# Two graph layers on one core: when the next batch of x is loaded, and into which buffer

## The chip, the cores and the metric

The kernel runs on one core of a Trainium2 chip. The metric is the device time in microseconds of that core, the median of three runs. A profiled execution was taken beside them; all stage times below are from it, and it was itself longer than the timed runs (1170.05 us against 1118.38 us).

## The reference

The input x is 32 batches of 512 nodes by 512 features, in float32. Two residual layers run one after the other, each with a layer norm and a ReLU in front.

```python
# --- layer 0 ---
h = jnp.maximum(_layernorm(x, axis=-1), 0.0)
y = jnp.einsum('nm,bmd->bnd', adj, h)
x = x + jnp.einsum('bnd,do->bno', y, weight) + bias
# --- layer 1 ---
h = jnp.maximum(_layernorm(x, axis=-1), 0.0)
q, k, v = h @ Wq + bq, h @ Wk + bk, h @ Wv + bv          # 8 heads of 64
scores = einsum('bqhd,bkhd->bhqk', q, k) / sqrt(64) + (1.0 - adj) * -1e9
out = einsum('bhqk,bkhd->bqhd', softmax(scores), v)
x = x + out.reshape(b, n, d) @ Wo + bo
```

The mask term is so large that, where each row of adj has a single largest entry, the softmax picks exactly one key for each query. Then layer 1 comes down to: take row idx(n) of h, multiply by Wv Wo, and add it to row n of x.

## The kernel before

The kernel first looks at adj and the weights on the chip and takes `single_path` if the softmax is sure to pick one key per row; with these inputs it does, and the other path plays no part in the time.

Work goes batch by batch, in a loop over b from 0 to B. Each turn of the loop runs three stages one after the other on TensorE. Each is one product of two 512 x 512 matrices by a scheme with seven products of half-sized blocks instead of eight (`product`, pieces p1, p5, u2, c11, c22, c12, c21):

- layer 0 of batch b (`layer0`, steps 0 to 6): y times w0, added onto x by VectorE (`take_onto`, L344),
- aggregation for batch b + 1 (`aggregate`, steps 7 to 13): adj times h, moved to yT by ScalarE and VectorE (L326, L324),
- layer 1 of batch b - 1 (`layer1`, steps 14 to 20): Wv Wo times the distinct rows that any query picked (352 columns), moved to zs (L337, L334).

Pieces of one product share accumulators. u2 and then c22 are added into the bank of p1, so the matmuls of c22 may start only when VectorE has taken u2 out of the bank (L344). That wait is the one named `PE mm L287 <- DVE x L344` below.

All other work hangs on these 21 steps by hand. `put(batch, step, f)` appends f to a step of this turn, and every engine runs its own instructions strictly in that order. Around the change:

- The results of layer 1 go back through memory. `put_z` (L545, L549) transposes zs and writes 11 groups of 32 rows to a buffer z in memory, in eight DMAs, at step 20 of one turn and step 0 of the next. `finish` (L553, step 1) adds the rows onto x with four indirect DMAs issued by GpSimd. `store` (L559, step 12) writes x to the output.
- The way out to layer 1 goes through memory too: `put_h` (L488, steps 9 and 11) writes h, `get_h` (L494, steps 12 and 15) gathers the picked rows with 11 indirect DMAs issued by GpSimd, and the next turn transposes them (`transpose_h`, L529, steps 5 to 8).
- GpSimd also computes the reciprocal square roots of the norms (`power`, L201), in the same queue as its DMAs.
- x lives in five buffers, batch b in `xs[b % 5]`. `load_x` (L253) issues four DMAs of 256 KB on the SyncE queue. The norm of batch b + 2 (`stats`, L194) reads the loaded x from step 9 on.

SyncE's queue carries, in one turn and in this order: the second half of z (step 0), the load of x, the two writes of h, the four stores, the first half of the next z (step 20). A DMA that must wait for another holds up all that stand behind it in the queue.

Of the kernel before, what the change touches and what calls it, by code (L numbers as in the profile page):

```python
# [26 lines left out]
def gnn_two_layers(ctx: ExitStack, tc: tile.TileContext, x, adj, w0, b0, wq, bq, wk, bk, wv, bv, wo, bo, out):  # L27
# [149 lines left out]
    with tc.If(single > P - 1) as cmp:  # L177
        single_path(tc, x, wv, bv, wo, bo, out, kept)
# [38 lines left out]
def single_path(ctx: ExitStack, tc: tile.TileContext, x, wv, bv, wo, bo, out, kept):  # L217
# [361 lines left out]
    with tc.manual_schedule():  # L579
# [6 lines left out]
        for b in range(B + 1):  # L586
            todo = [[] for _ in range(21)]

            def put(batch, step, f, *args):
                if 0 <= batch < B:  # L590
                    todo[step].append(lambda: f(batch, *args))

            put(b - 2, 15 if b == B - 1 else 1, finish)
            put(b + 2, 2, load_x)
            for step, i in ((0, 0), (1, 1), (2, 2), (3, 3)) if b > 0 else ((1, 0), (2, 1), (2, 2), (3, 3)):
                put(b + 1, step, h0_sum, i)
            put(b - 2, 14 if b == B - 1 else 0, put_z, 0, 6)
# [347 lines left out]
```

## Time and profile before

| What | Value |
|---|---|
| Timed runs | 1115.33, 1118.38, 1119.31 us; median 1118.38 us |
| Profiled execution | 1170.05 us, of which the trace spans 1168.3 us |
| TensorE (PE) busy | 1100.6 us, 94% of the span |
| VectorE (DVE) busy | 905.7 us, 78% |
| GpSimd (POOL) busy | 653.9 us, 56% |
| ScalarE (ACT) busy | 359.4 us, 31% |
| Granted TensorE clock, mean | 0.984 |
| DMA moved | 186.90 MB, mean 160 GB/s |

"Busy" is the time in which an engine has an instruction under way. A wait is written as who waited, an arrow, and what came last before it went on; "SPq" is the queue of SyncE, which only issues DMAs. In the tables by stretch, each engine's busy time and its number of instructions are followed by the granted clock, the busy share of the 16 DMA engines, and the rate that they moved.

### The profile page before, as it was taken

How to read it: one execution, taken by the hardware profiler on the slowest of the kernel's cores; microseconds unless marked ns; L12 is line 12 of the kernel's file. 1: busy time of each engine (PE TensorE's matmuls, PEld its weight loads, DVE VectorE, ACT ScalarE, POOL GpSimd, SP SyncE). 2: the span in 40 equal slices, each digit the busy share in tenths (PEclk: the TensorE clock that was granted, in tenths of full speed). 3: DMA queues.
4: the chain of work that ended last, by engine and by line, in shares of the span. 5: the costliest groups of instructions: out<-in, count | busy, mean ns of one | idle time of the engine just before them, and what ended most of it. 6: DMA issues, size and time to landing. Idle time of an engine off the chain costs nothing.

```text
span 1168.3 us, 15855 instructions
## 1 busy us (share of the span) xinstructions
PE 1100.6 (94%) x5408; PEld 957.8 (82%) x5408; DVE 905.7 (78%) x1859; ACT 359.4 (31%) x655; POOL 653.9 (56%) x584
## 2 busy tenths in 40 slices
PE   7999989999989999999999999899999999999885
PEld 3658878989978989888989888798998889998782
DVE  6879868878867878787888888687887878887760
ACT  4223313233313233323323332223333232233120
POOL 2146536655646765565765555566565656666443
PEclk9999989999989999999999999999999999999998
DMA  6414665655666665576665657566566756666438
GB/s 225 153 19 129 165 173 140 171 170 149 168 173 139 165 180 147 153 191 167 150 177 171 159 155 187 133 170 178 155 165 172 190 140 167 180 176 156 120 118 203
DMA packets 135146, 186.90 MB, mean 160 GB/s; under 512 B 17472, under 2 KB 61120, under 8 KB 135056
## 3 DMA queue, kind: packets, MB, share of 16 engines
q1 hardware_dynamic: 102320, 123.05, 31.0%
q0 software_dynamic: 29472, 56.47, 27.4%
q10 hardware_dynamic: 3264, 6.29, 1.5%
q8 instruction: 44, 0.72, 0.2%
q14 instruction: 46, 0.38, 0.1%
HBM read 96.28 MB, written 89.46 MB: 159 GB/s over the span
## 4 chain that ended last, share of the span: by engine, by line
PE 83%; DVE 6%; issue 3%; POOL 3%; ACT 1%; DMA 1%; another core or an unknown queue 1%; SPq 0%; POOLq 0%; ACTq 0%; DVEq 0%
PE mm L287 78%; DVE x L344 2%; POOL x L553 1%; PE mm L139 1%; PE mm L480 1%; PE mm L371 1%; DVE st L194 1%; DMA x<-in_x_dram 1%; PE mm L520 1%; ACT h L212 1%; POOL rstd L201 1%; POOL hc L494 1%; DVE h0s L266 1%; DVE yT L324 0%
## 5 line engine op out<-in xcount | busy, mean ns | idle before, releaser
L494 POOL DMA_INDIRECT hc<-hs,listed x341 | 356.2, 1045 | 261.9 <-DMA hs<-h 157.2
L344 DVE TENSOR_TENSOR x<-mm,x 128x512 f32<-128x512 f32 x217 | 149.6, 690 | 146.6 <-PE mm L287 107.7
L326 ACT COPY yT<-mm 128x512 f32<-128x512 f32 x124 | 71.8, 579 | 614.3 <-PE mm L287 478.3
L553 POOL DMA_INDIRECT x<-z,place x124 | 196.0, 1581 | 70.2 <-issue 47.9
L287 PE MATMUL mm<-w_t,sel 128*128 128x256 f32 x744 | 182.2, 396 | 37.9 <-DVE x L344 31.6
L212 ACT ACTIVATE h<-x,off,rstd 128x512 f32<-128x512 f32 x256 | 194.7, 807 | 48.2 <-DVE off L204 46.3
L287 PEld LDWEIGHTS mm<-w_t,sel 128*128 128x128 f32 x744 | 143.9, 196 | 67.5 <-DVE x L344 39.4
L201 POOL TENSOR_TENSOR rstd<-ve,mhalf 128x2 f32<-128x2 f32 (+1 forms) x97 | 97.2, 1002 | 156.9 <-DVE ve L200 151.8
L194 DVE BATCH_NORM_STATS2 st<-x 128x6 f32<-128x512 f32 x256 | 171.6, 670 | 8.4 <-DMA x<-in_x_dram 7.3
L287 PE MATMUL mm<-adjT_s,h0s 128*128 128x256 f32 x744 | 170.9, 379 | 0.4 <-ACT yT L326 0.2
L287 PEld LDWEIGHTS mm<-adjT_s,h0s 128*128 128x128 f32 x744 | 141.2, 190 | 20.3 <-ACT yT L326 1.2
L287 PE MATMUL mm<-hTs,wvo_t 128*128 128x176 f32 x720 | 117.8, 313 | 1.7 <-ACT zs L337 1.7
L287 PE MATMUL mm<-w_s,yT 128*128 128x256 f32 x496 | 117.2, 379 | 0.0
L287 PE MATMUL mm<-adjT,h 128*128 128x256 f32 x496 | 117.2, 379 | 0.0
L337 ACT ACTIVATE zs<-mm,cvo_c 128x176 f32<-128x176 f32 x248 | 87.4, 404 | 94.7 <-PE mm L287 60.4
L287 PEld LDWEIGHTS mm<-hTs,wvo_t 128*128 128x128 f32 x720 | 109.7, 190 | 2.8 <-ACT zs L337 2.8
L287 PEld LDWEIGHTS mm<-adjT,h 128*128 128x128 f32 x496 | 94.2, 190 | 13.2 <-issue 0.5
L287 PEld LDWEIGHTS mm<-w_s,yT 128*128 128x128 f32 x496 | 93.1, 190 | 11.7 <-issue 0.5
L458 DVE TENSOR_TENSOR x<-x,b_r 128x512 f32<-128x512 f32 x128 | 86.5, 677 | 0.0
L287 PE MATMUL mm<-hT,wvo 128*128 128x176 f32 x480 | 81.4, 313 | 0.0
L287 PEld LDWEIGHTS mm<-hT,wvo 128*128 128x128 f32 x480 | 75.3, 190 | 1.5
L324 DVE TENSOR_TENSOR yT<-mm,yT 128x512 f32<-128x512 f32 x93 | 63.5, 682 | 4.1 <-PE mm L287 2.7
(152 smaller groups left out, 1262.9 us busy)
## 6 DMA issues: line engine op xcount, KB each, us to landing
hs<-h SPq DMA_DIRECT2D x64, 512.0 KB
out_dram<-x SPq DMA_DIRECT2D x124, 256.0 KB
x<-in_x_dram SPq DMA_DIRECT2D x120, 256.0 KB
z<-zr SPq DMA_DIRECT2D x124, 96.0 KB
z<-zr SPq DMA_DIRECT2D x124, 80.0 KB
hc<-hs,listed POOLq DMA_INDIRECT x341
x<-z,place POOLq DMA_INDIRECT x124
x<-in_x_dram ACTq DMA_DIRECT2D x4, 256.0 KB
```

The source lines that it names most:

```text
L139: nc.tensor.matmul(ps, hs[0][:, m, d * P:(d + 1) * P], adjT[:, m, :], start=(m == 0), stop=(m == C - 1))
L194: self.nc.vector.bn_stats(st, self.src[:, self.chunks[i], :])
L201: self.nc.gpsimd.tensor_tensor(self.rstd, ve, self.mhalf[:, 0:n], ALU.pow)
L212: self.nc.scalar.activation(dst, src, AF.Relu, bias=self.off[:, i:i + 1], scale=self.rstd[:, i:i + 1])
L287: nc.tensor.matmul(bank[:, m, 0:half], lhs[:, k, m * P:(m + 1) * P], rhs[:, k, :], start=(first and m == 0 and k == 0), stop=(k == 1), ski ...
L324: nc.vector.tensor_add(dst, bank, dst)
L326: nc.scalar.copy(dst, bank)
L337: nc.scalar.activation(dst[:, m, :], bank[:, m, :], AF.Identity, bias=cvo_c[:, 2 * i + m:2 * i + m + 1])
L344: nc.vector.tensor_add(dst, bank, dst)
L458: nc.vector.tensor_add(X[b][:, c, :], X[b][:, c, :], b0_r)
L494: nc.gpsimd.indirect_dma_start(out=HC[b][:, s, :], out_offset=None, in_=HS[b].rearrange("n (q d) -> (n q) d", q=4), in_offset=bass.Indirec ...
L553: nc.gpsimd.indirect_dma_start(out=X[b][:, c, :], out_offset=None, in_=Z[b], in_offset=bass.IndirectOffsetOnAxis(ap=place[:, c:c + 1], axi ...
```

## The change

The load moves from step 2 to step 15 of the loop's turn, and fetches batch b + 3 instead of b + 2. Batch b + 3 goes into `xs[(b + 3) % 5]`, the buffer that batch b - 2 has just left at step 12, so each DMA of the load now follows the store of the same buffer by three steps; before, eleven steps lay between the two (the store at step 12, the load into that buffer at step 2 of the following turn). It is meant to take the load out of the stretch in which z is written and added onto x, and to put it where the DMA engines have less to do. The first two turns still load at step 2 as well, since nothing has been stored by then.

```diff
             put(b - 2, 15 if b == B - 1 else 1, finish)
-            put(b + 2, 2, load_x)
+            if b < 2:
+                put(b + 2, 2, load_x)
+            if b > 0:
+                put(b + 3, 15, load_x)
```

What is loaded, where it is kept, and all other work stay as they are. In the instruction order of the engines, only SyncE's differs: the four loads stand after the four stores instead of after z. VectorE keeps its order; its transpose before z (L545, the first half) waits for eight DMA semaphores in place of four.

## The prediction

> **What bounds the kernel now.** I read the clock view first (mean 0.984, so the clock is nearly full), then the engines' shares (TensorE 94%), then the table by stretch with one turn of the loop per row, because a mean over the span hides whether TensorE lacks work in every turn or in some.
>
> ```profile
> core 0: us, PE busy (x) PEld busy (x) DVE busy (x) ACT busy (x) POOL busy (x), PEclk, DMA share, GB/s
> 216.60:249.10 32.50, 32.50 (x170) 29.60 (x169) 27.27 (x57) 10.80 (x20) 20.11 (x18) 1.00 0.66 172
> 249.10:286.00 36.90, 34.53 (x171) 30.78 (x170) 27.58 (x57) 11.10 (x21) 21.18 (x19) 0.95 0.60 156
> 286.00:318.50 32.50, 32.50 (x170) 29.53 (x169) 27.59 (x57) 10.91 (x20) 21.11 (x18) 1.00 0.68 174
> 318.50:357.50 39.00, 35.92 (x171) 31.63 (x170) 27.76 (x57) 10.93 (x20) 20.09 (x18) 0.91 0.57 145
> 143.30:1073.90 930.60, 896.55 (x4538) 805.17 (x4537) 744.85 (x1513) 295.06 (x540) 556.44 (x486) 0.99 0.63 164
> ```
>
> The reader is to see two kinds of turn. In the good ones TensorE is busy for all of the 32.5 us: the turn is TensorE's own work and nothing else. The bad ones last 37 to 39 us with the same instructions. The last row holds 27 turns (4538 matmul records at 168 a turn): 930.6 / 27 = 34.47 us each, so 27 x (34.47 - 32.5) = 53 us of the profiled span are lost in bad turns.
>
> Next, where a bad turn loses it. The waits of TensorE between 143.3 and 1073.9 us, and the timeline of the bad turn that starts at 249.1:
>
> ```profile
> PE mm L287 <- DVE x L344: 27.4, 12, 3.2
> PE mm L287 <- issue: 6.2, 3, 3.8
> ```
>
> ```profile
> 250.86 3.62 PE L287 MATMUL mm<-w_t,sel 128*128 128x256 f32 x16
> ...
> 253.56 1.91 SPq L253 DMA_DIRECT2D x<-in_x_dram  x4
> ...
> 254.94 0.69 DVE L344 TENSOR_TENSOR x<-mm,x 128x512 f32<-128x512 f32 x1 [2.59 <-PE mm L287]
> ...
> 257.83 0.69 DVE L344 TENSOR_TENSOR x<-mm,x 128x512 f32<-128x512 f32 x1 [1.60 <-remote]
> ...
> 258.58 3.00 PE L287 MATMUL mm<-w_t,sel 128*128 128x256 f32 x8 [2.37 <-DVE x L344]
> ```
>
> TensorE waits for VectorE, yet VectorE is itself idle: it waits 2.59 us for TensorE. The 16 matmuls from 250.86 on are p5 (eight) and u2 (eight); at 0.216 us from start to start, p5's last one ends near 250.86 + 8 x 0.216 + 0.16 = 252.75. VectorE gets the word at 254.94, over 2 us later, and the one of u2 at 257.83 although u2 was over near 254.5. "remote" is what the view writes when no instruction ended shortly before. So the word of the matmuls' end comes late; no engine is short of time. The half-clock stretches follow such waits (0.95 and 0.91 in the two bad rows) and make up the rest of the 53 us.
>
> **Is this in the timed runs?** The profiled execution took 1170.05 us, the timed median is 1118.38: 51.7 us less. The bad turns account for 53 us. Taking them out of the profiled time gives 1170.05 - 53 = 1117, within 1.4 us of the timed median. I therefore hold that the timed runs have almost none of these late words, and that they spend their 27 middle turns at TensorE's 32.5 us.
>
> Last, where the load stands among the transfers of a good turn's worth of time:
>
> ```profile
> 515.57 2.43 SPq L488 DMA_DIRECT2D hs<-h  x2
> 518.10 2.67 SPq L559 DMA_DIRECT2D out_dram<-x  x4
> 530.83 3.77 SPq L549 DMA_DIRECT2D z<-zr  x8
> 534.64 1.90 SPq L253 DMA_DIRECT2D x<-in_x_dram  x4
> ```
>
> ```profile
> 519.00:523.00 4.00, 4.00 (x22) 3.64 (x21) 3.93 (x10) 0.59 (x1) 1.45 (x2) 1.00 0.93 349
> 523.00:531.00 8.00, 8.00 (x55) 7.92 (x54) 7.48 (x15) 5.53 (x12) 6.56 (x7) 1.00 0.17 46
> 531.00:537.00 6.00, 6.00 (x29) 5.29 (x28) 2.89 (x5) 0.23 (x1) 4.66 (x5) 1.00 0.74 196
> 537.00:541.00 4.00, 2.51 (x12) 1.89 (x11) 2.93 (x6) 0.00 (x0) 1.72 (x1) 1.00 0.72 242
> 541.00:549.00 8.00, 8.00 (x39) 7.04 (x38) 7.25 (x17) 2.12 (x4) 5.40 (x4) 1.00 0.85 124
> ```
>
> The load now follows z and falls between 535 and 541, just ahead of the four accumulating DMAs of `finish` (541 to 549, 0.85 busy). From 523 to 531, in layer 1, the DMA engines are 0.17 busy. The change moves 1 MB from the crowded stretch into that hole.
>
> **What the Trainium skill says.** "DMA: Bandwidth & Descriptors", section "Issuing engines are not separate DMA queues": transfers from SyncE and GpSimd run on the same 16 DMA engines and interleave. The trace agrees: one busy share covers z, x and the gathers, and GpSimd's indirect DMA takes 1.42 us beside the load at 290.35 where it takes 0.95 us without. The same page, section "Two DMAs through the same engine are not ordered": a DMA that depends on an earlier one has to wait, on the issuing engine, for that one's semaphore, so queue order alone isn't enough. This is the wait that the load will have on the store; the trace of before can't show it, since no load there waits so. "TensorE: Matmul & The Clock Gate", section "Part 1: The HAM clock gate": the clock goes to half after a window of about 3.4 us in which TensorE was idle. The trace shows half clock right after TensorE's waits of 2 to 3 us, so it agrees roughly: waits somewhat shorter than the page's window were enough.
>
> **The change, part by part.**
>
> Removed at step 2: four DMA issues, 1.90 us of SyncE's queue, which is idle from 536.5 to 549.5 anyway. The 1 MB leaves the DMA engines before `finish`. GpSimd waits 2.27 us ahead of the first DMA of `finish` (539.15 against the last gather's end at 536.9). With z's last DMA issued at 534.16 and nothing behind it, z should land up to 2 us sooner, so `finish` may start near 537 and end near 545 instead of 546.5. Who gains: the reciprocal roots (L201) behind it in GpSimd's queue, and VectorE, which waits for them 33.6 us in 42 waits in the middle turns. But TensorE waited only 2.0 us in all for the VectorE work behind that (L324). Worth to the end: 0 to 2 us.
>
> Added at step 15: the load waits in SyncE's queue for each store to land. The stores are issued from 518.1 to 520.8 and the fast traffic ends near 523; the Trainium skill's DMA page ("Anatomy of one DMA") puts about 2 us of fixed cost on a transfer, so as an estimate the first lands at 521 to 522 and the last at 523 to 525. Issues then run to about 525 or 526 and, at the 349 GB/s of the row above, 1 MB takes 3 us: landed by 530. Behind the load in the queue stands only the first half of z, ready at 530.8. It is not held up: 5 us of room. If the stores took twice as long, still 2.
>
> Moved into the hole: the 11 gathers run from 521.2 to 536.9 beside it. At 1.42 - 0.95 = 0.47 us more for the six issued in those 8 us, that is up to 2.8 us later on GpSimd; those issued beside the load at step 2 today get it back (three in the turn at 286). Net 0 to 1.5 us, against the 2.27 us that GpSimd idles before `finish`: hidden. The last gather is needed by the third transpose at 513.4 in the turn before, 547 in this one, some 9 us after its issue: hidden.
>
> The data: read from step 9 of the next turn on instead of seven steps after its issue. VectorE doesn't wait for x in the middle turns today, so the longer lead is worth nothing. The four more semaphores on L545 cost VectorE an instruction or two of 0.05 us (the length of the ones that it has now), before p1 is taken; u2 can start only after that, with about 0.8 us to spare in the good turn (p1 taken by 288.61, u2's first matmul at 287.72 + 8 x 0.216 = 289.45). Hidden.
>
> Sum on the path of the timed run: minus 0 to 2 us, plus 0. I take 1.9 us, most of the upper end, since some late words may be left in the timed runs as well.
>
> **The rivals.**
>
> Faster by over 0.5%: the late words are caused by the crowd of z, gathers and x, and the timed runs still have some. For it: they come in layer 0's first pieces, just where z is written, turn after turn. Against it: in the turn shown, the word of p5 was late before the first load was issued (253.56), so z and not x would be the cause, and z stays; and the room is small. 1170.05 - 53 leaves 1.4 us; if the profiled head and tail hold losses too (the last 94 us have a mean clock of 0.92, some 7 us), the room is 1.4 + 7 = 8 us. All of it: 1118.4 - 8 = 1110 us.
>
> Slower by over 0.5%: the gathers and the load disturb each other more than 0.47 us a DMA, `finish` starts later, the roots behind it come late, VectorE stops in front of them with layer 0's pieces and aggregation's behind, and TensorE follows. For it: VectorE is over 0.9 busy in layer 1 and has little room to catch up. Against: 2.27 us of slack at `finish`. If 0.3 us a turn got through: 28 x 0.3 = 8 us, 1127 us; at 1 us a turn, 1146 us.
>
> Slower by SyncE: the load's wait for the store holds z. That needs 5 us more than estimated; each further us would then come onto z and `finish`. For 1 us a turn again 1146 us; I give it little.
>
> **How the numbers follow.** No measurable change 0.56: the prediction, 1118.4 - 1.9 = 1116.5 us. Faster by over 0.5% (below 1112.8) 0.31, centred on 1110. Slower by over 0.5% (above 1124) 0.13, both slower rivals together. The range from 1106 to 1124 leaves out half of the extreme end of the faster case and nearly all of the slower ones, about 2 in 10.
>
> **What would show it.** Right: the load issued between 521 and 526 on the same scale (some 6 us after the stores begin), the DMA share of the hole near 0.5, `finish` starting up to 2 us sooner after z, no wait of VectorE for x, and good turns still at 32.5 us. Bad turns may become fewer in the profiled run without the timed ones following. Wrong: good turns of other than 32.5 us; a timed gain beyond 8 us, which would mean that the late words are in the timed runs too; or z issued late behind the load, or GpSimd's roots late behind gathers that take over 1.4 us.

## The result, and the profile after

The changed kernel takes 1112.97 us (median; 1112.71 to 1113.45), the kernel before beside it 1118.65 us (1115.33 to 1119.31). The ratio is 0.9956 with a 95% interval from 0.9936 to 0.9976: a gain of 0.44%, clear of noise, and just inside the half per cent that was called no measurable change (the interval reaches to both sides of it). 1116.5 us was predicted. In this text, medians are of all runs and ratios of the fast ones alone (at most 1.5% above the fastest of their kernel); for chip D below, where most runs are slower than that, the median of the fast ones is given.

The profiled execution of the changed kernel took 1112.71 us, 57 us less than that of the kernel before (1170.05 us). That is not the effect of the change. The experiments below show that one and the same kernel differs by this much from one group of runs to another, each group on its own chip. So the two profiles can be compared in the order and the places of their transfers, but not in their length, nor in how often TensorE waits.

By stretch (length, busy time and count of each engine, clock, DMA share, rate), a turn of the loop and the 27 middle turns of the changed kernel:

```profile
699.30:731.90 32.60, 32.60 (x171) 29.67 (x170) 27.69 (x57) 10.92 (x20) 21.06 (x18) 1.00 0.66 174
142.00:1024.60 882.60, 881.27 (x4537) 798.12 (x4537) 744.28 (x1513) 294.81 (x540) 565.19 (x487) 1.00 0.66 172
```

882.6 / 27 = 32.69 us a turn, so what the middle turns lose against 32.5 us is 5 us in all. The waits of TensorE in the middle turns say the same; of the 27.4 us for L344 nothing is left:

```profile
PE mm L287 <- ACT yT L326: 0.3, 1, 0.3
```

This is not the work of the change: on another chip the changed kernel still waits 25.4 us for L344 (below).

SyncE's queue over one turn (start, length, what):

```profile
488.56 2.44 SPq L488 DMA_DIRECT2D hs<-h  x2
491.09 2.67 SPq L559 DMA_DIRECT2D out_dram<-x  x4
494.15 2.67 SPq L253 DMA_DIRECT2D x<-in_x_dram  x4
503.80 3.79 SPq L549 DMA_DIRECT2D z<-zr  x8
```

The load starts 3.1 us after the stores do, and z follows 7 us after the load's last issue. The queue's own waits show what the new dependence costs it:

```profile
SPq L253 <- DMA out_dram<-x: 46.8, 104, 2.0
```

That is 46.8 / 104 = 0.45 us for each of the load's DMAs that waited, at most 2.0, in a stretch where nothing else stands in the queue. And the DMA engines by stretch, to be set beside the stretches of before in the prediction:

```profile
494.00:499.00 5.00, 5.00 (x34) 4.90 (x33) 4.93 (x12) 2.50 (x7) 4.14 (x4) 1.00 1.00 349
499.00:503.50 4.50, 4.50 (x31) 4.45 (x30) 4.00 (x8) 3.36 (x6) 3.39 (x5) 1.00 0.20 61
503.50:510.00 6.50, 6.50 (x32) 5.72 (x31) 5.48 (x9) 0.48 (x2) 5.28 (x5) 1.00 0.61 161
```

The hole behind the stores is filled (share 1.00 from 494 to 499), the stretch of z has dropped from 0.74 to 0.61. In layer 0 the words of the matmuls' end come on time in this profile:

```profile
505.16 0.65 DVE L344 TENSOR_TENSOR x<-mm,x 128x512 f32<-128x512 f32 x1
...
506.72 0.69 DVE L344 TENSOR_TENSOR x<-mm,x 128x512 f32<-128x512 f32 x1 [0.32 <-PE mm L287]
...
508.45 0.69 DVE L344 TENSOR_TENSOR x<-mm,x 128x512 f32<-128x512 f32 x1 [0.44 <-PE mm L287]
```

p1, p5 and u2 are taken 1.6 to 1.7 us apart, the pace of eight matmuls (8 x 0.216). In the bad turn of before it was 3.9 and 2.9 us; there p1 was taken at 251.08, and p5 and u2 at 254.94 and 257.83, as the prediction shows:

```profile
251.08 0.67 DVE L344 TENSOR_TENSOR x<-mm,x 128x512 f32<-128x512 f32 x1
```

### The profile page after: what moved, and what is told of

Same layout as the page of the kernel before. It is cut to its first block, busy times and chain, and to the rows that moved or that the text cites. A ratio compares the mean times of both kernels' runs of the same rounds, so it can differ in the third digit from the quotient of the medians.

```text
span 1110.9 us, 15992 instructions
## 1 busy us (share of the span) xinstructions
PE 1083.0 (97%) x5408; PEld 950.4 (86%) x5408; DVE 905.1 (81%) x1859; ACT 359.2 (32%) x655; POOL 662.4 (60%) x584
## 4 chain that ended last, share of the span: by engine, by line
PE 87%; DVE 5%; POOL 2%; issue 2%; DMA 1%; ACT 1%; SPq 0%; POOLq 0%; ACTq 0%; DVEq 0%
PE mm L287 83%; PE mm L139 1%; POOL x L553 1%; PE mm L480 1%; DVE st L194 1%; PE mm L371 1%; POOL rstd L201 1%; DVE x L344 1%; DMA x<-in_x_dram 1%; DVE yT L324 1%; DVE zs L334 0%; SPq L549 0%; DMA z<-zr 0%; ACT zs L337 0%; DVE mv L195 0%
## 5 line engine op out<-in xcount | busy, mean ns | idle before, releaser
L494 POOL DMA_INDIRECT hc<-hs,listed x341 | 367.7, 1078 | 261.1 <-DMA hs<-h 156.2
L326 ACT COPY yT<-mm 128x512 f32<-128x512 f32 x124 | 71.5, 577 | 546.0 <-PE mm L287 489.7
L553 POOL DMA_INDIRECT x<-z,place x124 | 192.9, 1556 | 47.6 <-issue 38.8
L344 DVE TENSOR_TENSOR x<-mm,x 128x512 f32<-128x512 f32 x217 | 149.6, 689 | 86.2 <-PE mm L287 86.2
L201 POOL TENSOR_TENSOR rstd<-ve,mhalf 128x2 f32<-128x2 f32 (+1 forms) x97 | 104.9, 1081 | 114.2 <-DVE ve L200 111.6
L287 PE MATMUL mm<-w_t,sel 128*128 128x256 f32 x744 | 171.1, 379 | 0.8 <-DVE x L344 0.8
L287 PEld LDWEIGHTS mm<-w_t,sel 128*128 128x128 f32 x744 | 141.1, 190 | 20.9 <-DVE x L344 1.8
```

The source lines that it names most:

```text
L201: self.nc.gpsimd.tensor_tensor(self.rstd, ve, self.mhalf[:, 0:n], ALU.pow)
L287: nc.tensor.matmul(bank[:, m, 0:half], lhs[:, k, m * P:(m + 1) * P], rhs[:, k, :], start=(first and m == 0 and k == 0), stop=(k == 1), ski ...
L326: nc.scalar.copy(dst, bank)
L344: nc.vector.tensor_add(dst, bank, dst)
L494: nc.gpsimd.indirect_dma_start(out=HC[b][:, s, :], out_offset=None, in_=HS[b].rearrange("n (q d) -> (n q) d", q=4), in_offset=bass.Indirec ...
L553: nc.gpsimd.indirect_dma_start(out=X[b][:, c, :], out_offset=None, in_=Z[b], in_offset=bass.IndirectOffsetOnAxis(ap=place[:, c:c + 1], axi ...
```

## The experiments

Twelve runs in four groups, each group on one chip together with the kernel before. The chips are called A to D here; on which one the first measurement was made isn't known, and no chip served two groups, so a difference between chips can't be told from one between the times at which they ran. Below, "late word" means a wait of VectorE for a matmul that was already over; "loss" is the time above TensorE's own.

**The kernel before, unchanged** (chip A). No edit. Is the difference between 1170 and 1118 us made by the profiler?

> The kernel before, unchanged, profiled and timed once more. Theory R (the late words of the matmuls' end belong to one disturbed profiled execution and are not the rule): the new profile spans about 1117 us, with good turns of 32.5 us and far less than 53 us lost, and the 5.7 us by which the changed kernel is faster show up as small waits of TensorE in layer 0's first pieces or behind roots that come late. Theory L (late words are the kernel's own under a profile, whenever the load follows z): the profile again spans 1150 to 1180 us while the timed runs stay at 1115 to 1120. Ratio to before under both: 1.000 within 0.003.

Measured: 1158.45 us (1155.21 to 1166.98), ratio 1.0001 (0.9972 to 1.0031); the kernel before in the same group 1160.96 us. Neither theory: the timed runs took as long as the profiled one (1158.42 us). So here the timed runs have the late words too, and 1118 us belongs to the first group of runs. The same kernel run twice more:

> The kernel before once more, for its profile on the same chip as the changed kernel's. Theory z and theory crowd: same span as the timed runs of this call, within 1%; late words (VectorE waiting over 1 us for a matmul that was over) in most turns if this is a chip with 1150 us or more, in none or few if it takes 1115 to 1119.

> The kernel before a third time, for a profile on whichever chip this is. If it takes 1115 to 1119 us here, as in the first timed runs: theory rare late words says that the profile spans 1113 to 1117 us, most turns last 32.5 us, and two to four turns in layer 0 are 1 to 3 us longer, 5 to 6 us in all. If it takes 1150 to 1170 us, as on the other chips: late words in most turns, 40 to 55 us in all, and the first timed runs stay without a profile of their own.

On chip B 1159.09 us (ratio 0.9996, 0.9972 to 1.002), on chip D 1174.93 us (ratio 1.002, 0.997 to 1.0071). The low level of the first runs never came back, so the kernel before has no profile at that level.

The times expected for the next three runs were written for a kernel before of 1118 us; on chip A, at 1160 us, only the ratios can be held against them.

**Without the load** (chip A).

```diff
         X[b] = xs[b % 5]
+        if b > 4:
+            return
         for c in range(C):
```

> The kernel before without the loads of batches 5 to 31: those batches work on what the buffer holds, so their numbers mean nothing; all other work stays. Theory crowd (the load's traffic beside z and the accumulating DMAs is what costs): as fast as the changed kernel or slightly faster, 1110 to 1113 us. Theory lead (the data came too late, or the queue order alone matters): 1110 to 1113 as well, since nobody waits for data. Theory elsewhere (the gain comes from what the load does in its new place or from the different waits of the transpose before z): 1117 to 1119 us, no gain.

Measured: 1155.69 us, ratio 0.9949 (0.9925 to 0.9972). Leaving the load out altogether is worth 0.5%, as much as the change brought in the first group, as the theories crowd and lead both said (1110 to 1113 us of 1118.65 is 0.992 to 0.995). The remaining loss, some 40 us above the changed kernel's first time, is not the load's.

**The old traffic put back into the changed kernel** (chip A; `load_spare` issues the same four DMAs as `load_x`, into `spare`).

```diff
...
             if b > 0:
                 put(b + 3, 15, load_x)
+            if b > 1:
+                put(b + 2, 2, load_spare)
```

> The changed kernel with a second load of x in the old place, behind z, into a spare buffer that nobody reads. Theory crowd: the gain is lost, 1117 to 1120 us, and waits of TensorE come back in layer 0. Theory lead (what counted was that the data arrive earlier): stays at 1113 us, since the real load keeps its new place.

Measured: 1166.21 us, ratio to before 1.0031 (1.0005 to 1.0058). The real x arrives as early as in the changed kernel, and the gain is gone. So the longer lead was worth nothing; what counts is the load's traffic in its old place, where z and the gathers are under way.

**The load between the two halves of z** (chip A; the edit as it stands against the kernel before).

```diff
-            put(b + 2, 2, load_x)
+            if b < 2:
+                put(b + 2, 2, load_x)
...
                 put(b - 1, 20, put_z, 6, S)
+            if b > 0:
+                put(b + 3, 20, load_x)
```

> Batch b + 3 loaded as far ahead as in the changed kernel, but issued between the two halves of z (after z's first half at step 20, before its second at step 0). Theory crowd: no gain or slower than before, 1118 to 1130 us, because the second half of z is issued about 2 us later and shares the engines with 1 MB. Theory lead: 1113 us, since the data come a turn ahead.

Measured: 1211.31 us, ratio 1.0431 (1.0376 to 1.0486), beyond what was expected. SyncE's queue in this run, and the waits of TensorE, GpSimd and VectorE:

```profile
511.04 1.77 SPq L549 DMA_DIRECT2D z<-zr  x4
512.86 1.89 SPq L253 DMA_DIRECT2D x<-in_x_dram  x4
514.86 3.68 SPq L549 DMA_DIRECT2D z<-zr  x4
```

```profile
PE mm L287 <- ACT yT L326: 34.2, 22, 3.2
PE mm L287 <- DVE x L344: 32.1, 23, 2.3
...
POOL x L553 <- DMA z<-zr: 100.1, 21, 5.4
...
DVE off L204 <- POOL rstd L201: 87.2, 53, 4.4
```

The second half of z leaves 2 us later, and a second place of waiting appears, in aggregation (L326). What is added is for the most part of another cause than late words: GpSimd now waits 100.1 us for z, the first DMA of the finish starts 11.8 us after layer 0's first matmul (522.34 - 510.53) instead of 7.8, the roots behind it come late (VectorE waits 87.2 us for them; 36.5 in the kernel before on chip B), and with them ScalarE, which norms h and moves yT in one queue. The prediction had this chain under "slower by SyncE". The same 1 MB of load, with the same long lead, moves the time by -0.65% (chip B, next) or +4.3%, depending on what it holds up and stands beside.

**The changed kernel on a second chip** (chip B). No edit.

> The changed kernel, unchanged, beside the kernel before on one chip. On a chip where the kernel before takes 1150 to 1170 us: theory crowd (the load's traffic at z makes the words of the matmuls late) says that the late words go with the load, so 1113 us, ratio 0.96; theory z (z and the gathers make them late by themselves, the load adds little, as the run without loads at ratio 0.995 suggests) says a ratio of 0.990 to 0.997, 1150 to 1157 us. On a chip where the kernel before takes 1115 to 1119 us both say 0.995.

Measured: 1153.12 us against 1159.5 us, ratio 0.9935 (0.9909 to 0.9961): theory z, that is, z and the gathers make the words late by themselves. The change brings 0.65% here, more than the half per cent called no measurable change; the interval overlaps the one of the first group. The waits of TensorE and of VectorE in the middle turns, first of the kernel before on this chip:

```profile
PE mm L287 <- DVE x L344: 26.4, 14, 2.9
...
DVE x L344 <- remote: 11.5, 13, 3.0
```

and of the changed kernel:

```profile
PE mm L287 <- DVE x L344: 25.4, 14, 3.5
...
DVE x L344 <- remote: 7.8, 9, 3.0
```

Most late words are still there. The clock view gives a span of 1159.7 us at a mean clock of 0.986 before and 1145.2 us at 0.993 after, so what the clock costs falls from 0.014 x 1159.7 = 16.2 us to 0.007 x 1145.2 = 8.0 us: fewer waits are followed by half clock. Two profiled executions differ by more than the change (the runs of the changed kernel spread from 1140.98 to 1157.91 us here), so this is a reading, not a proof.

**Without z's writes, and without the gathers** (both on the kernel before, chip B; in the first, all batches keep one buffer z).

```diff
...
-        for q in range(4):
+        for q in range(4 if b == 0 else 0):
             nc.sync.dma_start(rows[q][:, s0:s1, :], ZR[b][32 * q:32 * q + 32, s0:s1, :])
```

```diff
     def get_h(b, first, last):
+        if b > 0:
+            HC[b] = HC[0]
+            return
         if first == 0:
```

> The kernel before without the writes of z after the first batch: every later batch adds the z of batch 0, so the result means nothing; the load stays behind the place of z. Theory z: late words vanish and the time is TensorE's own, 1108 to 1114 us on any chip. Theory crowd: the load is still there beside the gathers, half of the loss stays. Theory gathers (GpSimd's indirect DMAs make the words late): the loss stays.

> The kernel before without the gathers of h after the first batch: layer 1 works on the rows of batch 0, so the result means nothing. Theory gathers: 1108 to 1114 us on any chip. Theory z: the loss stays, since z is written as before, 1150 us or more where the kernel before takes 1160; GpSimd then reaches the first DMA of the finish earlier, which is worth a few us at most.

Measured: without z 1125.62 us, ratio 0.9701 (0.9641 to 0.9761). Its waits, and SyncE's queue:

```profile
PE mm L287 <- DVE x L344: 12.1, 14, 2.9
...
DVE x L344 <- remote: 9.2, 10, 3.0
```

```profile
502.62 2.66 SPq L559 DMA_DIRECT2D out_dram<-x  x4
505.68 2.67 SPq L253 DMA_DIRECT2D x<-in_x_dram  x4
```

This run changed more than was meant. With z's writes gone, nothing holds the load in SyncE's queue: it is issued 3.1 us after the stores, in the hole, as in the changed kernel. So the run is best set beside the changed kernel on this chip (1153.12 us), from which it differs in little but z, and theory crowd, which needed the load in its old place, isn't tested by it. Late words come without z's writes: 10 waits for "remote", as long as 3.0 us, against 13 in the kernel before and 9 in the changed one.

Without the gathers 1109.53 us, ratio 0.9577 (0.9523 to 0.9631), and no wait of TensorE is listed in the middle turns at all, although z and the load are issued as before. The gathers are needed for the loss; z makes it larger. Theory z, in the sense of z alone as the cause, falls.

**The gathered bytes without GpSimd's issuing** (chip C).

```diff
-            nc.gpsimd.indirect_dma_start(
-                out=HC[b][:, s, :], out_offset=None, in_=HS[b].rearrange("n (q d) -> (n q) d", q=4),
...
+                nc.sync.dma_start(HC[b][:, s, :],
+                                  HS[b].rearrange("n (q d) -> (n q) d", q=4)[s * P:(s + 1) * P, :])
```

> The kernel before with the gathers of all batches but the first replaced by 11 plain DMAs of the same 64 KB each on SyncE's queue (rows in order instead of the picked ones, so layer 1's result means nothing). Theory issue (it is GpSimd's issuing of indirect DMAs, beside z, that makes the matmuls' words late): 1108 to 1114 us on any chip, as without gathers. Theory traffic (it is the bytes of the gathered rows on the DMA engines beside z and the load): the loss stays, within 1% of the kernel before.

Measured: 1109.77 us, ratio 0.9552 (0.9518 to 0.9585), and again no wait of TensorE is listed in the middle turns. SyncE's queue:

```profile
492.07 5.60 SPq L499 DMA_DIRECT2D hc<-hs  x11
501.80 3.77 SPq L553 DMA_DIRECT2D z<-zr  x8
505.62 1.88 SPq L253 DMA_DIRECT2D x<-in_x_dram  x4
```

This is what theory issue said: the same bytes, fetched by SyncE's queue, do no harm. But the edit also moved them in time. All 11 are issued by 497.67, 4 us before z, while GpSimd's gathers are spread over some 16 us and the last of them run beside z, in layer 0. Theory traffic, that it is the bytes at that moment, is therefore not refuted. Nor can it be told whether it is GpSimd's instruction or the queue that serves it; the four accumulating DMAs of the finish, which GpSimd issues too, were kept. What the run does show: with the load in its old place, beside z, and no gathers there, nothing is lost.

**Two attempts at a faster kernel** (chip C), on the changed one: z whole and later, with the finish at step 9; and z whole at step 0, with the finish where it was. The edit of the first (the second has its last lines too, and `put_z` at step 0):

```diff
-            put(b - 2, 15 if b == B - 1 else 1, finish)
+            put(b - 2, 15 if b == B - 1 else 1 if b == B else 9, finish)
...
-            put(b - 2, 14 if b == B - 1 else 0, put_z, 0, 6)
+            put(b - 2, 14 if b == B - 1 else 0 if b == B else 4, put_z, 0, 6 if b >= B - 1 else S)
...
-            if b < B and b != B - 2:
+            if b == B - 1:
                 put(b - 1, 20, put_z, 6, S)
```

> The changed kernel with z written whole at step 4, after GpSimd's gathers have been issued, and the finish at step 9, for all batches but the last three. Theory overlap (late words come while gathers and z run together): 1110 to 1116 us on any chip, faster than the changed kernel wherever that takes more. Against it: the finish's accumulating DMAs then run up to the store and may hold SyncE's queue at step 12; then the load and z come late, and it is no better than the changed kernel.

> The changed kernel with z written in four DMAs at step 0 instead of eight at steps 20 and 0. Theory overlap: the four DMAs still run beside the last gathers, so the loss mostly stays: ratio to before 0.985 to 1.000 on a chip where that takes 1150 us or more. Theory count (the number of DMAs and their issues in that stretch is what counts): half of the loss goes, ratio 0.975 to 0.985 there.

Measured: z later 1179.75 us, ratio 1.0153 (1.0124 to 1.0183); z whole at step 0 1154.59 us, ratio 0.9932 (0.9905 to 0.9959), the same as the changed kernel on chip B within the intervals. In the first, the finish and then the gathers stand before the norm's roots (L201) in GpSimd's queue.

```profile
519.83 1.55 POOL L553 DMA_INDIRECT x<-z,place  x1 [0.31 <-issue]
521.69 1.27 POOL L494 DMA_INDIRECT hc<-hs,listed  x1 [0.30 <-issue]
...
525.51 1.05 POOL L201 TENSOR_TENSOR rstd<-ve,mhalf 128x4 f32<-128x4 f32 x1
```

```profile
DVE off L204 <- POOL rstd L201: 76.4, 51, 3.2
...
DVE x L344 <- remote: 26.4, 18, 1.6
```

VectorE waits 76.4 us for the roots instead of 32.7 (the changed kernel, chip B), SyncE's stores wait for the finish (192.9 us in that run's queue waits), and TensorE gains a wait for zs (16.7 us). And the late words stay: 18 waits for "remote", although z is now issued after the gathers. So theory overlap, in which late words need z beside the gathers, falls, and the order of GpSimd's queue was made worse. In the second, four DMAs beside the last gathers do no less than eight; theory count falls.

## Why the prediction was right, and where it was not

The time and the verdict came out: 1116.5 us predicted, 1112.97 measured, inside the range. That the two are so near is luck. The one term that the sum rested on, a finish up to 2 us sooner, was worth nothing, and the 5.7 us that were gained most likely came by the way of the faster rival (late words made by the crowd of z, gathers and x), which the runs on chips A and B bear out. The verdict held by 0.06%; on chip B the gain was 0.65%.

Layer 0's first matmuls and the first DMA of the finish in a good turn, before and after:

```profile
285.99 1.89 PE L287 MATMUL mm<-w_s,yT 128*128 128x256 f32 x8
...
293.80 1.59 POOL L553 DMA_INDIRECT x<-z,place  x1 [0.30 <-DMA x<-in_x_dram]
```

```profile
699.34 1.89 PE L287 MATMUL mm<-w_s,yT 128*128 128x256 f32 x8
...
707.13 1.58 POOL L553 DMA_INDIRECT x<-z,place  x1 [0.30 <-issue]
```

Step by step:

- **The hole and the collision.** Right. The load went into the hole, and on chip A the runs without the load (0.9949) and with the dummy load (1.0031) show from both sides that its old place accounts for a gain of this size. The hole was filled somewhat more than "near 0.5": 1.00 for 5 us, then 0.20, a mean of 0.62.
- **The load's wait for the store.** Right. The four issues stood at 3.1 to 5.7 us after the stores began, where 521 to 526 of the prediction is 2.9 to 7.9 us; z had 7 us to spare instead of 5. The estimate took its 2 us of fixed cost from the Trainium skill's "DMA: Bandwidth & Descriptors", whose section "Anatomy of one DMA" gives it for DMAs issued by GpSimd; in the profile after, a store issued by SyncE lands 3.3 us after its issue (the median), which comes to the same as the estimate's 521 to 522.
- **The finish up to 2 us sooner.** Wrong; it starts no sooner. In a good turn of before it follows layer 0's first matmul by 293.80 - 285.99 = 7.8 us, and in a good turn after by 707.13 - 699.34 = 7.8 us. In both, the finish follows the last gather by 0.30 us: what it stands behind is the gathers in GpSimd's queue and not z. The 2.27 us of idle time that I read as z's came from a turn of 34.3 us and don't stand for a good one.
- **"Is this in the timed runs?"** Wrong in its reason. I took 1170 against 1118 us for the profiler's doing. On chips A, B and D the kernel before takes 1158 to 1175 us timed, and its profiled run lies within its timed ones; in the first group the profiled run of the changed kernel (1112.71 us) is as fast as the timed ones. So the profiler isn't needed to explain the 51.7 us; a difference between chips, or between the times at which they ran, is the reading that fits all groups, though where the first profile came from isn't known. That the first group's timed runs have few late words may still be true. The room of up to 8 us derived from it held only because the measurement was made at that level. There, 5.7 of the 8 us were gained.
- **"z would be the cause, and z stays."** Half right. The late word before the load's first issue did show that the load isn't the cause. But z isn't either: without the gathers both are harmless, and without z's writes late words still come. The load in its old place makes the loss larger, by 0.5% of the time.
- **"Slower by SyncE."** Rightly given little, since z had 7 us to spare. Where the load does hold z, between its halves, the chain named there is what costs 4.3%.
- **The lead, the four more semaphores, the slower gathers.** Right that they cost nothing. GpSimd's gathers take 1.078 us on average after, 1.045 before (the groups' means), which is 0.4 us a turn and hidden. The 1.42 us beside the load was not the load's doing: in the same turn of before, a gather of 1.34 us starts at 288.69, ahead of the load's first issue. The room of the last gather was 547 - 535.93 = 11 us after its issue, not 9, which changes nothing.

What stays open: how the gathers delay the words from TensorE to VectorE, whether by GpSimd's issuing or by their bytes at that moment, why the waits come in layer 0 and seldom elsewhere, and why the first group's changed kernel shows none of them. That the first group's gain comes from the same late words is argued, not shown: no profile of the kernel before exists there.

## What to carry to other kernels

When a profiled run and the timed runs disagree, run the same kernel again, profiled and timed, on one chip before explaining the difference: here times and profile agreed as soon as they came from one group. Where an engine waits for a matmul that is long over, look also at which transfers are being issued at that moment. When moving a transfer, ask what stands beside it and behind it: the same 1 MB moved the time by -0.65% in a hole behind the stores and by +4.3% between two halves of another transfer, whose readers then came late. And after taking a transfer out, look where those behind it in the queue have gone: without z's writes the load moved by itself.

## What the runs showed of the hardware that was not expected

- One kernel, the one before, took 1118.65, 1159.5, 1160.96, 1161.09 and 1172.49 us as the medians of five groups, while the same kernel beside itself in a group gave ratios of 0.9996 to 1.002. In the four groups of the experiments the granted clock of its runs lay near 0.98 to 0.99; for the one at 1118.65 us it isn't recorded.
- Eleven gathers of 64 KB a turn, issued by GpSimd, cost 50 us (1159.5 us with them, 1109.53 without), although VectorE, which reads their data (L529), is idle ahead of it for 0.3 us in all in the middle turns of before. The same bytes by SyncE's queue, issued before z, cost nothing (1109.77 us).
- The end of a matmul can reach the waiting engine 2 to 3 us late while TensorE goes on with the next piece in time. In the bad turn shown, c11 was started in time at 254.32, right behind a u2 whose word arrived at 257.83. Late words come with z's writes left out (waits up to 3.0 us) and with z moved behind the gathers too (up to 1.6 us); in the two runs without GpSimd's gathers of h no wait of VectorE for a matmul in layer 0 is over 1.0 us in the middle turns.

```profile
254.32 1.89 PE L287 MATMUL mm<-w_s,yT 128*128 128x256 f32 x8
```
